# Attention and scan of a four-layer image network as one stream: query chunks of 256 instead of 512, shared 4 KB pieces and shared PSUM banks

## The chip, the cores and the metric

The kernel runs on one core of a Trainium2 chip. A core has a matrix engine (TensorE), an engine for element-wise work and scans (VectorE), one for activation functions (ScalarE), a fourth for general work (GpSimd), a sync engine (SyncE) that issues most transfers, and 16 DMA engines that carry them. Each engine works off its own queue of instructions in the order written; semaphores make one engine wait for another. Operands lie in SBUF, 128 partitions wide; TensorE writes into PSUM, from which VectorE and ScalarE read.

The metric is device microseconds (us) of one execution, the median of the runs.

## The reference, cut to what matters

Four layers work in turn on x of 4 samples x 128 channels x 64 x 64 pixels (4096 positions a sample), all in float32. Only layers 0 and 1 are touched by the change.

```python
# layer 0, per sample: q, v are 128 x 4096; w, b are one number per query position
k      = q / clip(norm(q), 1e-4)
logits = k.T @ q                                   # 4096 keys x 4096 queries
sparse = relu(logits - mean(logits, axis=0) * w + b)
mask   = sparse != 0
attn   = clip(softmax(logits * sparse, axis=0) * mask, 1e-8)
y      = v @ attn                                  # 128 x 4096
x1     = leaky(conv3x3(y) + lin_b) + x

# layer 1, per sample: a selective scan over the 4096 positions, 128 channels x 64 states
u      = layernorm(x_mamba) * gamma + beta
delta  = softplus(dt_raw @ W_dtr + b_dtr)
h[l]   = exp(delta[l] * A) * h[l-1] + delta[l] * B[l] * u[l]
y      = sum_n h[l] * C[l] + u * D
x2     = x1 + (y + silu-gated depthwise conv) @ W_out

# layer 2, per sample: attention with a rank-1 logit, softmax(f_i * g_j), times values
# layer 3: one scan in each direction over all 4 samples' 16384 positions, 256 channels x 16 states
```

## The kernel before, in words

**Order of the program.** The samples run one after the other: `layer0(0)`, `layer1(0)`, `layer0(1)`, `layer1(1)` and so on (`body`, the last function), then layer 2 of the last sample and layer 3. Each stage opens its own pools of SBUF and PSUM and closes them at its end. Nearly every instruction is issued through `InOrder`, whose line L111 the profile therefore shows; it keeps the order on each engine as written. So instructions are told apart by the names of their tiles.

**Layer 0, turns.** A sample's queries are cut into 8 chunks of 512. A *turn* is one block of 256 keys by 512 queries, that is a tile of 128 x 1024 elements (two key blocks of 128 side by side); a chunk has U = 16 turns, a sample S = 128. In turn `i` of the loop these are written, each for a turn of its own, so that they overlap:

- `weights(i)`: VectorE, e = max(t, 0) x lg, reads the logits' PSUM pair.
- `logits(i+2)`: TensorE, two matmuls of 512 columns into one of two PSUM pairs `lg`. A float32 matmul makes two passes of the matrix engine.
- `above(i+1)`: VectorE, t = lg + ncut, the row of thresholds of this chunk.
- `floored(i-18)`: VectorE, t = max(t, fl), where fl is the softmax floor of a chunk, which is known when all 16 turns of the chunk are through: hence the lag of LAG = U + 2 = 18 turns, in which the t tiles are kept.
- `shifted(i)`: GpSimd, e = e - bound; then ScalarE, exp(e). On every second turn ScalarE also takes the sign of a t.
- `beside(i)`: two ScalarE exponentials of 512 with a running sum (`junk`), the row weights of layer 2 of the sample before (not for sample 0).
- `product(i-19)`: TensorE, two matmuls of 512 columns that add into the PSUM tile `acc`.
- `masked(i-1)`: t = mask(t) x e; on odd turns GpSimd, on even turns VectorE.
- `sums(i-2)` on even turns: TensorE adds e over the keys into `zs`.

At a chunk's end `scales` turns zs into the floor and into the scale 1/z: a copy of zs on ScalarE, a matmul with `floor_c` for fl, a small transpose, a reciprocal on VectorE, a spread back by TensorE into `misc`, a copy on ScalarE. `image` multiplies acc by that scale into a padded picture, and `convolved` makes the 3x3 convolution with nine matmuls (taps). `thresholds` make ncut and bound of the next chunk: four matmuls through `misc`, with a ScalarE or VectorE step behind each, and the two steps of bound, one on GpSimd (`top`) and one on VectorE (`top_b`). Convolution, thresholds and values (v) go through a queue: per turn up to two steps that are not TensorE's and one that is.

PSUM (eight banks of 512 float32 columns): two pairs `lg`, and one bank each for `misc`, `zs`, `fl` and `acc`.

After turn S the loop goes on for LAG + 2 turns with only floored, product, image and convolution; beside them runs `first_tokens`, which prepares the first window of layer 1 and stores it (`u1`, `parts1`).

**Layer 1, tiles.** A sample has 4 windows of 1024 positions, each with 64 *tiles* of 128 partitions (16 states of 8 channels) x 1024 positions; 256 tiles a sample. `scan_stream` writes per tile: TensorE's spread of du over the partitions (`db`), ScalarE's decay exp (`da`) from a row that a DMA brings in, VectorE's db x b_rep and the scan itself (`h`), GpSimd's h x c_rep (`p`), and every four tiles TensorE's sums of p into `total`. Of each four tiles one is *apart*: GpSimd makes its x, ScalarE its decay in PSUM. Beside the tiles run, through a queue with `tile` and `late`, the preparation of the next window (`tokens_of`), the depthwise convolution, the finishing of the window before (`done`), layer 2's attention of the sample before (`attend`), and in the last window the queries and keys of the next sample (`tokens`). After the last tile `beside` and the queue are worked off.

Of the kernel before, what the change touches and what calls it, by code (L numbers as in the profile page):

```python
# [16 lines left out]
P = 128  # L17
IMG = 64
# [96 lines left out]

class Net:


    def __init__(self, ctx, tc, ins, out):
# [21 lines left out]
        self.u1 = dram.tile([P, self.T], F32, name="u1", tag="u1")  # L141
        self.parts1 = dram.tile([3, P, self.T], BF16, name="parts1", tag="parts1")
# [160 lines left out]
    def weights12(self):  # L303
# [24 lines left out]
        self.diagD1 = self.diagonals(pool, "diagD1", self.D_param, 1)[:, 0, :]  # L328

# [6 lines left out]
    def layer0(self, b):  # L336
# [4 lines left out]
        NT = L // P  # L341
        U = NT // 2
        S = NCH * U
        LAG = U + 2
        with self.pool("l0", 1) as big, self.pool("l0t", 2) as tmp, self.pool("l0a", LAG + 3) as ap, \
                self.pool("l0e", 4) as ep, self.pool("l0q", 2, True) as ps2, self.pool("l0p", 1, True) as ps1:
            k = big.tile([P, L], F32, name="k", tag="k")
            vT = big.tile([P, NT, P], F32, name="vT", tag="vT")
            ypad = self.padded_image(big, "ypad")
            ksum = self.ksum  # L350

            def misc(name, rows=P):
                return ps1.tile([rows, NB], F32, name=name, tag="misc")

            def row(name, bufs=2, rows=P):
                return tmp.tile([rows, NB], F32, name=name, tag=name, bufs=bufs)

            def pair():
                return ps2.tile([P, 2, NB], F32, name="lg", tag="lg")

            def key(c):
                s = bass.ts(c, NB)
                sp.dma_start(out=k[:, s], in_=self.k0[:, s])

            for c in range(0 if b else NCH):
                s = bass.ts(c, NB)
                xq = row("xq")
                nc.sync.dma_start(out=xq, in_=self.ins["x"][b, :, s])
                ps = pair()
                nc.tensor.matmul(ps[:, 0, :], self.q_wT, xq, start=True, stop=True)  # L370
                q = row("q")
                nc.scalar.activation(q, ps[:, 0, :], AF.Identity, bias=self.q_b)
                nc.sync.dma_start(out=self.q0[:, s], in_=q)
                sq = row("y", 1)
                nc.gpsimd.tensor_tensor(sq, q, q, ALU.mult)
                nc.tensor.matmul(ps[0:1, 1, :], self.ones[:, 0:1], sq, start=True, stop=True)
                own = row("own")
                nc.scalar.activation(own[0:1, :], ps[0:1, 1, :], AF.Sqrt)
                nc.sync.dma_start(out=self.norms[:, s], in_=own[0:1, :])

                n_ps = ps1.tile([P, NB], F32, name="n_ps", tag="zs")
                for i in range(4):
                    nc.tensor.matmul(n_ps[:, i : i + 1], sq[:, bass.ts(i, P)], self.ones[:, 0:1], start=True, stop=True)
                inv = tmp.tile([P, 4], F32, name="inv", tag="inv")
                nc.scalar.activation(inv, n_ps[:, 0:4], AF.Sqrt)
                nc.vector.tensor_scalar(inv, inv, 1e-4, None, ALU.max)
                nc.vector.reciprocal(inv, inv)
                inv_ps = ps1.tile([P, NB], F32, name="inv_ps", tag="fl")
                for i in range(4):
                    nc.tensor.matmul(  # L390
                        inv_ps[:, bass.ts(i, P)], inv[:, i : i + 1].to_broadcast([P, P]), self.ident,
                        start=True, stop=True,
                    )
                nc.vector.tensor_tensor(k[:, s], inv_ps, q, ALU.mult)
                nc.vector.tensor_reduce(ksum[:, c : c + 1], k[:, s], AX.X, ALU.add)
            if b == 0:
                self.weights0()
            kbar = tmp.tile([P, 1], F32, name="kbar", tag="kbar")
            nc.vector.tensor_reduce(kbar, ksum, AX.X, ALU.add)
            nc.vector.tensor_scalar(kbar, kbar, 1.0 / L, None, ALU.mult)  # L400
            kbar_rep = self.replicated(tmp, "kbar_rep", kbar)
            self.exp_tables(act)

            queue = Queue()
            held = {}

            def values(c):
                def load():
                    held["xv"] = row("xq")
                    sp.dma_start(out=held["xv"], in_=self.ins["x"][b, :, bass.ts(c, NB)])  # L410

                def v():
                    held["v"] = misc("v_ps").rearrange("p (a b) -> p a b", b=P)
                    for i in range(4):
                        pe.matmul(held["v"][:, i, :], held["xv"][:, bass.ts(i, P)], self.v_wT, start=True, stop=True)

                def plus():
                    dve.tensor_tensor(
                        vT[:, 4 * c : 4 * c + 4, :], held["v"], self.v_b.unsqueeze(1).to_broadcast([P, 4, P]), ALU.add,
                    )  # L420

                return [load, on_pe(v), plus]

            qs, ncut, bound = {}, {}, {}

            def thresholds(c):


                s = bass.ts(c, NB)

                def load():
                    qs[c] = held["q"] = row("q")
                    sp.dma_start(out=qs[c], in_=self.q0[:, s])
                    held["own"] = row("own")
                    sp.dma_start(out=held["own"], in_=self.norms[:, s].to_broadcast([P, NB]))

                def into(rows, lhsT, key):
                    def go():
                        held["ps"] = misc("th_ps", rows)
                        pe.matmul(held["ps"], lhsT, held[key], start=True, stop=True)  # L440
                    return on_pe(go)

                def hidden():
                    held["h"] = row("h", 1, 64)
                    act.activation(held["h"], held["ps"], AF.Prelu, bias=self.w1_b, alpha=0.2)

                def mean():
                    held["m"] = row("m", 1)
                    act.copy(held["m"], held["ps"])

                def times():
                    dve.scalar_tensor_tensor(held["m"], held["ps"], self.lw2_b, held["m"], ALU.add, ALU.mult)

                def cut():
                    ncut[c] = row("ncut")
                    dve.scalar_tensor_tensor(ncut[c], held["ps"], self.bw2_b, held["m"], ALU.add, ALU.subtract)

                def top():
                    bound[c] = row("bound")
                    pool.tensor_tensor(bound[c], held["own"], ncut[c], ALU.add)  # L460

                def top_b():
                    dve.scalar_tensor_tensor(bound[c], bound[c], 0.0, held["own"], ALU.max, ALU.mult)

                return [
                    load, into(64, self.w1_T, "q"), hidden, into(P, kbar_rep, "q"), mean,
                    into(P, self.lw2_rep, "h"), times, into(P, self.bw2_rep, "h"), cut, top, top_b,
                ]

            def both(t):  # L470
                return t.unsqueeze(1).to_broadcast([P, 2, NB])

            lg, t, e, zs, acc, floor, scale = {}, {}, {}, {}, {}, {}, {}

            def logits(i):
                if i < S:
                    c, m = divmod(i, U)
                    lg[i] = pair()
                    for j in range(2):
                        pe.matmul(lg[i][:, j, :], k[:, bass.ts(2 * m + j, P)], qs[c], start=True, stop=True)  # L480

            def above(i):
                if i < S:
                    t[i] = ap.tile([P, 2, NB], F32, name="t", tag="t")
                    dve.tensor_tensor(t[i], lg[i], both(ncut[i // U]), ALU.add)

            def weights(i):
                e[i] = ep.tile([P, 2, NB], F32, name="e", tag="e")
                dve.scalar_tensor_tensor(e[i], t[i], 0.0, lg.pop(i), ALU.max, ALU.mult)

            def shifted(i):
                if i and i % 2 == 0:

                    act.activation(t[i - 1], t[i - 1], AF.Sign)
                pool.tensor_tensor(e[i], e[i], both(bound[i // U]), ALU.subtract)
                act.activation(e[i], e[i], AF.Exp)

            def sums(i):

                c, m = divmod(i, U)  # L500
                if m == 0:
# [214 lines left out]

# [1365 lines left out]
```

## Time and profile before

Three runs took 10496.26, 10499.89 and 10501.62 us; the median is 10499.89. The profiled execution took 10494.9 us by its span, the time from the first to the last instruction; the page lists no other time of its own, so its execution is set 5.0 us below the median.

| | |
|---|---|
| span of the profiled execution | 10494.9 us, 91078 instructions |
| VectorE busy | 9159.8 us, 87% |
| TensorE busy | 8443.5 us, 80% |
| GpSimd busy | 8156.1 us, 78% |
| ScalarE busy | 6387.1 us, 61% |
| DMA | 1552.75 MB, mean 148 GB/s |

The stages as the starts of tiles show them (layer 0 from the first to the last t <- lg, ncut; layer 1 from the first scan's start to the last's):

| sample | layer 0, from - to (us) | length | gap | layer 1, from - to (us) | length | gap to the next sample |
|---|---|---|---|---|---|---|
| 0 | 63.1 - 686.6 | 623.5 | 99.4 | 786.0 - 1645.0 | 859.0 | 40.0 |
| 1 | 1685.0 - 2323.4 | 638.4 | 100.4 | 2423.8 - 3307.5 | 883.7 | 39.6 |
| 2 | 3347.1 - 3984.5 | 637.4 | 100.6 | 4085.1 - 4966.3 | 881.3 | 39.0 |
| 3 | 5005.3 - 5642.2 | 636.9 | 100.1 | 5742.2 - 6608.9 | 866.7 | |

Layer 2 of the last sample lies between 6609 and 6953 us, layer 3's scans between 6953 and 10415.

How to read what the prediction shows: a group's line gives engine, operation, output <- inputs, partitions x elements, number of instructions, then busy time and mean nanoseconds of one, then the engine's idle time before them and what ended it. A line of a stretch gives, engine by engine, the busy time and in brackets the number of instructions, then TensorE's granted clock (1.0 is full speed), the busy share of the DMA engines and what they moved. A line of the timeline gives the start, the duration, engine and operation. "PE", "DVE", "ACT", "POOL" and "SP" are TensorE, VectorE, ScalarE, GpSimd and SyncE.

### The profile page before, as it was taken

The page shows a single profiled execution, that of the slowest core. Times are in us where ns is not written, and L with a number is a line of the kernel's source. Part 1 is how long each engine was busy: PE and PEld are TensorE (multiplying, and loading weights), DVE is VectorE, ACT ScalarE, POOL GpSimd, SP SyncE. Part 2 cuts the span into 40 slices and gives each one's busy share as a digit, 9 for nine tenths or more (in the row PEclk, how much of TensorE's full clock was granted, in tenths as well). Part 3 has the DMA queues.
Part 4 walks back from the last instruction along what each step waited for, and adds up shares of the span by engine and source line. Part 5 has one row for each costly group of instructions (what it writes and reads, how often), then busy time and mean ns, then how long its engine had stood idle before and what let it go on. Part 6 is the DMA issues. An engine that isn't in the chain of part 4 may idle for free. (4 is left out here: it accounts for less than half of the span.)

```text
span 10494.9 us, 91078 instructions
## 1 busy us (share of the span) xinstructions
PE 8443.5 (80%) x28013; PEld 3021.6 (29%) x28088; DVE 9159.8 (87%) x6318; ACT 6387.1 (61%) x9576; POOL 8156.1 (78%) x3574
## 2 busy tenths in 40 slices
PE   8996667997887997887898887877777777777775
PEld 3331213332223333223333222322222222222221
DVE  7869998887998886999886999359999999999996
ACT  3334545666665665666665776456666666677765
POOL 6758896766887775888674888149999999989986
PEclk9997788998998999998999999888988989888886
DMA  1018882007885005887102888158888888888896
GB/s 37 12 37 201 194 194 85 18 14 189 211 203 149 15 14 129 201 213 191 33 16 63 206 211 200 32 133 199 207 198 206 204 202 208 215 223 224 228 227 176
DMA packets 512313, 1552.75 MB, mean 148 GB/s; under 512 B 84017, under 2 KB 91825, under 8 KB 511825
## 3 DMA queue, kind: packets, MB, share of 16 engines
q1 hardware_dynamic: 511824, 1546.92, 58.9%
q8 instruction: 223, 3.65, 0.2%
q14 instruction: 266, 2.17, 0.1%
HBM read 1349.40 MB, written 137.48 MB: 142 GB/s over the span
## 5 line engine op out<-in xcount | busy, mean ns | idle before, releaser
L111 POOL TENSOR_TENSOR p<-h,c_rep 128x1024 f32<-128x1024 f32 x2048 | 4807.9, 2359 | 734.8 <-DVE h L111 673.7
L111 DVE TENSOR_TENSOR_SCAN h<-da,carry,db 128x1024 f32<-128x1024 f32 x1536 | 3603.4, 2346 | 200.5 <-ACT da L111 17.8
L111 PE MATMUL db<-parts,sel 96*128 96x512 bf16 x4096 | 1401.5, 428 | 1460.3 <-DVE h L111 1408.2
L111 ACT ACTIVATE da<-row,A 128x1024 f32<-128x1024 f32 x1536 | 1761.1, 1147 | 359.4 <-DMA row<-d 341.0
L111 DVE TENSOR_TENSOR db<-b_rep,db 128x1024 f32<-128x1024 f32 x1536 | 1853.5, 1207 | 112.1 <-PE db L111 92.0
L111 POOL TENSOR_TENSOR e<-e,bound 128x1024 f32<-128x1024 f32 x512 | 1241.3, 2427 | 573.5 <-DVE e L111 573.0
L111 POOL TENSOR_TENSOR x<-row,b_rep 128x1024 f32<-128x1024 f32 x512 | 1208.8, 2361 | 123.8 <-DMA row<-d 122.8
L111 DVE TENSOR_TENSOR_SCAN h<-db,carry,x 128x1024 f32<-128x1024 f32 x512 | 1194.9, 2334 | 62.9 <-ACT db L111 35.3
L111 PE MATMUL total<-p,gather 128*32 128x512 f32 x8192 | 1225.7, 719 | 9.8 <-POOL p L111 9.8
L111 ACT ACTIVATE db<-db,A 128x1024 f32<-128x1024 f32 x512 | 555.3, 1085 | 1080.6 <-PE db L111 1026.5
L111 ACT ACTIVATE e<-e 128x1024 f32<-128x1024 f32 x512 | 540.9, 1057 | 1051.9 <-POOL e L111 1051.8
L111 PEld LDWEIGHTS <-sel 96*128 96x128 bf16 x4096 | 309.6, 101 | 3002.0 <-DVE h L111 2017.3
L111 PE MATMUL lg<-q,k 128*128 128x512 f32 x2048 | 1021.5, 623 | 106.5 <-DVE e L111 98.3
L111 PE MATMUL acc<-t,vT 128*128 128x512 f32 x2048 | 964.1, 595 | 3.3 <-DVE t L111 3.3
L111 PE MATMUL acc<-e,values 128*128 128x512 f32 x1536 | 854.9, 648 | 88.8 <-ACT e L111 62.9
L111 DVE TENSOR_TENSOR t<-lg,ncut 128x1024 f32<-128x1024 f32 x512 | 624.5, 1220 | 288.1 <-PE acc L111 264.0
L111 ACT ACT_TABLE_LOAD x617 | 791.6, 1283 | 38.8 <-DMA r<-y 12.3
L111 ACT ACTIVATE e<-gq,below,fcol 128x512 f32<-128x512 f32 x768 | 610.2, 805 | 87.0 <-PE acc L111 86.7
L111 POOL TENSOR_TENSOR t<-t,e 128x1024 f32<-128x1024 f32 x256 | 610.4, 2384 | 45.4 <-ACT t L111 45.4
L111 ACT ACTIVATE junk<-gp,ntop,fcol 128x512 f32<-128x512 f32 x768 | 619.5, 807 | 30.4 <-DMA gp<-g 17.7
L111 ACT COPY carry<-h 128x1 f32<-128x1 f32 x2048 | 373.5, 185 | 416.4 <-DVE h L111 411.4
L111 DVE SCALAR_TENSOR_TENSOR e<-t,lg 128x1024 f32<-128x1024 f32 x512 | 618.5, 1208 | 1.2
(259 smaller groups left out, 9927.5 us busy)
## 6 DMA issues: line engine op xcount, KB each, us to landing
row<-d SPq DMA_DIRECT2D x2048, 512.0 KB
parts<-split SPq DMA_DIRECT2D x912, 64.0 KB
b_rep<-bc SPq DMA_DIRECT2D x96, 512.0 KB
c_rep<-bc SPq DMA_DIRECT2D x96, 512.0 KB
d<-delta SPq DMA_DIRECT2D x76, 384.0 KB
r<-y SPq DMA_DIRECT2D x48, 512.0 KB
xq<-in_x SPq DMA_DIRECT2D x72, 256.0 KB
res<-x SPq DMA_DIRECT2D x32, 512.0 KB
```

Of the source, the lines that this page charges most:

```text
L111: return self.tc.keep_in_program_order(method(*args, **kwargs))
```

## The change

All samples' layers 0 and 1 become one stream (`layers01`). What changes:

- **Memory.** One class, `Memory`, holds SBUF as 44 pieces of 4 KB a partition, which a tile takes and gives back in the order of a queue, and PSUM as two pairs, one bank `a` (misc), one bank `b` and two banks `cd` (the scan's total). In layer 0 acc and fl are the two halves of bank b; zs and the rz of the scale lie in the two banks of cd, in one tile. In layer 1 bank b takes layer 2's acc.
- **Chunks.** A query chunk is Q = 256. A turn is four key blocks of 128 by 256 queries, still 128 x 1024; a chunk has U = 8 turns, a sample still S = 128, and LAG is 10. Thresholds put two results of 256 columns into one bank. The picture is a ring of three padded strips of four rows, whose edges ScalarE copies.
- **Order in a turn.** product, fl's matmul and the two steps of the scale on TensorE now stand ahead of logits; sums follow every turn; the steps of the scale have fixed turns (m = 1 and 2) instead of the queue; thresholds of the next chunk start in turn m = 1 at the head of the queue.
- **Ends beside beginnings.** Turns S and later (floored, product, image, convolution) are written inside the first tiles of layer 1 (`side`). First tokens run in the queue from turn 58, every third turn. The scan begins (rows, first spread) in turn S - 8. The last sums and `done` of the scan before are written in turns 0 to 2 of the next sample's layer 0. Values, keys, mean key, the first chunk's thresholds of the next sample are made in the last window of layer 1; values there get their bias by a matmul with one row and are copied by ScalarE.
- **Beside.** The row weights of layer 2 are exponentials of 1024 from turn 16 on, one a turn and two in each fifth. `attend` starts at tile 21 and doubles up when i % 6 == 2. Layer 1's work of the first window beside the scan starts at tile 16 instead of 2. The nine diagonals of the depthwise convolution are made once and stored.

```diff
+class Memory:
+    def take(self, name, shape=None, dtype=F32):
+        i = self.left.pop(0)
+        t = self.slots.tile(list(shape or [P, self.net.T]), dtype, name=name, tag=f"slot{i}")
...
+    def give(self, *tiles):
+        for t in tiles:
+            self.left.append(self.at.pop(id(t))[0])
...
+        Q = 256
+        NC, RQ, NT = L // Q, Q // IMG, L // P
+        J = self.T // Q
+        U = NT // J
+        S = NC * U
         LAG = U + 2
...
+        def sums(i):
+            m = i % U
+            if "zs" not in bank:
+                both_banks = mem.total("zs_rz")
+                bank["zs"], bank["rz"] = both_banks[:, 0:Q], both_banks[:, NB:]
...
+        def floored(i):
+            dve.tensor_tensor(t[i], t[i], both(bank["fl"]), ALU.max)
...
+        def floor_of(c):
+            if "b" not in bank:
+                bank["b"] = mem.other("acc_fl")
+                bank["acc"], bank["fl"] = bank["b"][:, 0:Q], bank["b"][:, Q:]
+            pe.matmul(bank["fl"], self.floor_c, zcopy.pop(c), start=True, stop=True)
...
+        def turn_of(i):
+            c, m = divmod(i, U)
+            w = i - LAG
...
+            if i in due:
+                d = due.pop(i)
+                image(d)
...
+            if i < S:
+                weights(i)
+            if 0 <= w - 1 < S:
+                product(w - 1)
...
+            if 0 <= w < S and w % U == 0:
+                floor_of(w // U)
+            scaled = U < i <= S + 2
+            if scaled and m == 1:
+                run[0][1]()          # turned
+            if scaled and m == 2:
+                run[0][3]()          # spread
+            logits(i + 2)
+            above(i + 1)
+            if 0 <= w < S:
+                floored(w)
+            if scaled and m == 1:
+                run[0][2]()          # inverted
+            if i and i <= S and (i - 1) % 2:
+                signs(i - 1)
+            if i < S:
+                shifted(i)
+            beside(i)
+            if scaled and m == 2:
+                run[0][4]()          # copied
+            if 0 < i <= S:
+                masked(i - 1)
+                for o in range(0 if i == 3 else i - 1, i) if i >= 3 else ():
+                    sums(o)
+            if i and i <= S and i % U == 0:
+                run[0] = scales(i // U - 1)
+                run[0][0]()          # kept
+            if i < S and m == 0 and c + 1 < NC:
+                given(c + 1)
+            if m == 1:
+                if i < S and c + 1 < NC:
+                    queue.first(thresholds(c + 1))
...
+            rounds(2 if i < LAG else 1)
...
+    def layers01(self):
...
+            for b in range(self.B):
+                after = self.layer0(b + 1, mem) if b + 1 < self.B else None
+                prior, Y = Y, self.layer1(b, mem, Z, after)
+                for i in range(Z.S):
+                    if prior and i == 0:
+                        prior.scan.last()
...
+                    if i >= 58 and i % 3 == 1:
...
+                        if early:
+                            Z.queue.add(early.pop(0))
+                    if i == Z.S - 8:
+                        Y.scan.begin()
+                    Z.front(i)
+                Y.scan.ready()
+                for i in range(Y.scan.n):
+                    Y.scan.tile(i)
+                if after:
+                    after.start()
+                    Y.kept["queue"] = after.queue
...
+            tail = kept["before"]
+            if tail:
+                tail.tail(tail.S + i)
+                tail.rounds(1)
+                if tail.over():
+                    tail.close()
+                    kept["before"] = None
             beside(i)
...
         net.weights012(pool)
-        for b in range(net.B):
-            net.layer0(b)
-            net.layer1(b)
+        net.layers01()
```

(The four words behind # name the steps that `scales` returns and are not in the code.)

## The prediction

> **What bounds the kernel now.** I read four views: the stretches of each stage, the groups of VectorE and GpSimd in one attention stage, the groups of VectorE in one scan stage, and the order of time inside an attention stage.
>
> ```profile
> core 0: us, PE busy (x) PEld busy (x) DVE busy (x) ACT busy (x) POOL busy (x), PEclk, DMA share, GB/s
> 1645.00:1695.00 50.00, 31.15 (x81) 10.89 (x80) 24.44 (x39) 10.51 (x20) 11.17 (x9) 0.80 0.41 138
> 1700.00:2320.00 620.00, 575.66 (x1729) 225.16 (x1730) 537.99 (x454) 411.93 (x706) 452.00 (x196) 0.98 0.05 15
> 2323.00:2430.00 107.00, 81.14 (x226) 34.02 (x225) 42.79 (x49) 36.17 (x49) 17.49 (x13) 0.90 0.32 84
> 2430.00:3300.00 870.00, 704.22 (x2575) 254.44 (x2577) 830.28 (x521) 598.52 (x919) 752.74 (x329) 0.92 0.84 208
> ```
>
> These are sample 1's stages. In the scans (2430 to 3300) VectorE is busy 95%: it is the bound, and what is added to it there is paid. In the attention (1700 to 2320) TensorE has 93% and VectorE 87%. In the 107 us and 50 us between, VectorE is busy 40 to 50%: that is what the change goes for. From the starts of the rows t<-lg and h<-da,carry,db: layer 0 runs 63.1-686.6, 1685.0-2323.4, 3347.1-3984.5, 5005.3-5642.2 (sum 2536); layer 1 runs 786.0-1645.0, 2423.8-3307.5, 4085.1-4966.3, 5742.2-6608.9 (sum 3491); the four gaps from 0 to 1 sum to 400, the three from 1 to 0 to 119. The rest of the 10494.9 us span is not touched.
>
> ```profile
> L111 DVE TENSOR_TENSOR t<-lg,ncut 128x1024 f32<-128x1024 f32 x122 | 148.8, 1220 | 73.4 <-PE acc L111 66.1 <-PE lg L111 7.3
> L111 DVE TENSOR_TENSOR t<-t,fl 128x1024 f32<-128x1024 f32 x108 | 130.5, 1209 | 1.3 <-PE fl L111 1.3
> L111 DVE SCALAR_TENSOR_TENSOR t<-t,e 128x1024 f32<-128x1024 f32 x61 | 102.8, 1685 | 6.0 <-ACT e L111 6.0
> L111 DVE SCALAR_TENSOR_TENSOR bound<-bound,own 128x512 f32<-128x512 f32 x7 | 18.5, 2649 | 0.0
> L111 POOL TENSOR_TENSOR e<-e,bound 128x1024 f32<-128x1024 f32 x123 | 297.6, 2421 | 133.4 <-DVE e L111 133.4
> L111 POOL TENSOR_TENSOR t<-t,e 128x1024 f32<-128x1024 f32 x61 | 145.4, 2383 | 11.2 <-ACT t L111 11.2
> ```
>
> Today t<-t,fl hardly waits (1.3 us in 108). The two VectorE operations with both inputs in SBUF, t<-t,e and bound, take 1.69 and 2.65 us on average although one of 1024 elements needs 1.2: they stand still while a GpSimd operation runs.
>
> ```profile
> 302.63 2.12 DVE L111 SCALAR_TENSOR_TENSOR t<-t,e 128x1024 f32<-128x1024 f32 x1
> 303.07 1.88 PE L111 MATMUL acc<-t,vT 128*128 128x512 f32 x4
> 311.06 1.16 PE L111 MATMUL rz_ps<-ident,rzt 128*128 128x128 f32 x8
> 313.05 1.22 DVE L111 SCALAR_TENSOR_TENSOR t<-t,e 128x1024 f32<-128x1024 f32 x1
> ```
>
> Four passes of 512 columns last 1.88 with a last one of 0.59, so 0.43 each; eight of 128 last 1.16 with 0.29, so 0.12 each. A pass of 256 is then 0.215 to 0.23. In the same view VectorE starts a 1024 operation every 1.13 us, one of 256 about every 0.35; GpSimd one of 1024 every 2.35; ScalarE's e<-e lasts 1.06.
>
> **The change, part by part.** I call one 128x1024 block of attention a turn; a sample has 128, as before, but a chunk is now 8 turns, not 16.
>
> 1. Gaps. 0 to 1: left are the rest of the last turns (3.4 to 6 us of VectorE), a selection matmul and a db product, so 10 each (bounds 4 and 20): 400 becomes 40, **-360**. 1 to 0: scan 2.3, GpSimd's p 2.4, the queued bound steps 1.1 and t<-lg 1.2, so 7 (3 to 15): 119 becomes 21, **-98**.
>
> 2. The attention's end in the scans. Ten t<-t,fl at 1.13, two images at 0.35 and some 5 of waits in the first tiles, where the scale's short steps pass through four engines: 17 a sample (12 to 30), all on VectorE and so on the path: **+68**. Its products (1.7 of TensorE a turn) lie under a scan tile's 3.4 us.
>
> 3. The scan's end in the first ten turns. These have no product and no t<-t,fl yet; GpSimd needs 2.35 + 2.35/2 = 3.5 a turn. The last window's finish brings 6.7 of VectorE and 5.3 of TensorE with waits of one for the other: 4.5 a turn (3.6 to 6), 45 in all, 44 for sample 0.
>
> 4. First tokens in turns 58 to 127. VectorE: two t minus split (the helper `less`), each 1.13 plus up to 2.3 behind GpSimd, and short ones: 7. All their matmuls share bank a with thresholds and convolution, each waiting for ScalarE to empty it: 18 more by eight chunks at about 2. So 25 (7 to 60).
>
> 5. The turn itself, other 117. TensorE: 16 passes at 0.215 for lg and acc, two groups of sums at 0.215 and two changes of operand at 0.1: 4.1; a chunk adds taps 3.9, thresholds 2.1, floor and scale 1.3: 40.2 per chunk, 5.0 a turn. VectorE: 24 operations at 1.13, four t<-t,e at 1.13, three of them held 1.2 by GpSimd, four of 256 at 0.35: 36.7, or 4.6 a turn. So neither load reaches today's 5.03 (638.4 / 127). The waits are what is new:
>  - zs and rz are one tile now. The built program makes the row sums of turn 2 wait until ScalarE has copied rz, behind that turn's exp: e<-t 1.2, e minus bound 2.4, exp 1.1, junk 1.4 (a 1024 row with 0.19 of read-out; two of 512 are 2.0), copy 0.4 = 6.5 after the turn's start. Then Prelu and mean, so the second threshold pair ends at 8.2, and the next turn's product, behind it in TensorE's queue, at 10.1. VectorE reached t<-t,fl at 6.8. Loss 3.3 a chunk, 1.9 for sample 0 (no junk).
>  - That t<-t,fl waits at all for a product comes from acc and fl being halves of one bank: in the built program each t<-t,fl waits for the product before it. 1.3 a chunk more, where TensorE is behind (turns 2 and 7).
>  - The GpSimd and the VectorE step of bound are issued in the same turn, an even one, where GpSimd first does e minus bound and t<-t,e: 2.35 + 2.35 + 0.65 after e<-t, while VectorE is through at 3.4: 3.3 a chunk, in which the whole queue of VectorE stands.
>  Sum 36.7 + 7.9 = 44.6, 5.6 a turn; sample 0 43.2, 5.4. Bounds: today a chunk of 16 turns takes 82.5 us (16 x 5.16 in mid-stage) against 79.0 of TensorE by the same passes, 4% over; TensorE's 5.0 with that 4% is 5.25, the lower end. If the queues never catch up and each wait costs twice, the turn is 36.7 + 15.8 over 8, 6.5; I put the range's end half-way, at 6.0. I take 5.6, since each of the three waits stands in the built program.
>  Layer 0: 44 + 117 x 5.4 + 25 = 701; the others 45 + 117 x 5.6 + 25 = 725: 2876 for 2536, **+340**.
>
> 6. Small: nine diagonals before the start, **+3** (today 2.8 a sample, in a gap). Values with bias rows and copies move to ScalarE in the last window: 7 of TensorE and 4.5 of ScalarE, under VectorE's scans; all paid it would be 11 a sample. Twice as many small transfers a chunk on SP: the DMA share in that stage is 0.05; uncovered, they would hold thresholds that have five turns of lead. Shared 4 KB pieces: the scans in the built program wait for the same producers as today, and GpSimd's p less often for TensorE; 0.1 a tile either way would be 100 in all.
>
> TensorE's passes decide part 5. The Trainium skill (TensorE: Matmul & The Clock Gate, Back-to-back issue gap) has 81 ns for 128 columns and 131 for 512 in real streams, which would make a pass of 256 half again as dear as half of one of 512. By it, an estimate, the turn would be 7.4 and the time near 11,300. The rows above, where 128 columns cost 0.12 and 512 cost 0.43, decide for the smaller price.
>
> Sum: -360 - 98 + 68 + 340 + 3 = **-47**. The profiled execution is 10494.9, the runs' median 5 above it; I add 5: 10,453, say 10,450.
>
> **Rivals.**
> - Faster still (0.2): the waits are absorbed by the slack between the queues, as t<-lg's 0.6 a turn is today, and the turn falls to TensorE's load, 5.25: 351 x -0.35 + 117 x -0.15 = -140, 10,310. For it: both loads are under 5.1. Against: each wait has a whole chain of four engines in order before it.
> - Slower (0.25): bank a. In turns 58 to 127 the first threshold pair waits until ScalarE, after exp and junk, has emptied the bank of a token or convolution step; 3 to 4 us in each of 35 chunks, carried on into the 3.3 above. Part 4 then costs 60 and not 25 a sample: +140, 10,590. It decides from 37 a sample on.
> - Slower (0.13): shared pieces. Row loads or scan outputs wait for a piece that is not free; 0.1 a tile, +100, 10,550. Against: the built program's waits.
>
> **How the numbers follow.** What a measurement can tell from no change is 0.2%, 21 us: faster means under 10,479, slower over 10,521. My case, a small gain, has 0.3 and the fast rival 0.2: 0.5 faster. 0.12 between, where part 5 is 0.1 a turn worse than computed (468 turns). Slower 0.38 by the two rivals or by a turn of 5.8 and more. Since signs are mixed: my case alone spans 10,380 to 10,479; the range of 8 in 10 goes from the fast rival, 10,310, to a turn of 6.0, 468 x 0.4 = 187 over, 10,640.
>
> **What will show it.** Gaps between last t<-lg and first scan under 20 us (else part 1 is wrong). The attention's turn between 5.3 and 5.7. VectorE's t<-t,acc_fl idle before it, on TensorE, by 4 to 5 us a chunk; bound idle on GpSimd by 3. Scan tiles as today but for the first ten. I am wrong if turns stay near 5.2 or pass 6, or if scan tiles change.

## The result, and the profile after

The changed kernel takes 10668.51 us (median, 10663.87 to 10675.88) against 10500.57 for the kernel before: a ratio of 1.016, 95% interval 1.0146 to 1.0175. It is slower by 168 us, where a gain of 50 was forecast, and 28 us above the stated range. The profiled execution spans 10662.1 us, 167 more than the one of before.

Taken apart at the starts of the same rows as before (layer 0 from the first to the last t<-lg, layer 1 from the first to the last scan, summed over four samples):

| part | before | after | difference | predicted |
|---|---|---|---|---|
| start of the first turn | 63 | 51 | -12 | +3 |
| layer 0, 4 x 128 turns | 2536 | 3019 | +483 | +340 |
| gaps from layer 0 to 1 | 400 | 38 | -362 | -360 |
| layer 1, tiles 0 to 31 | 452 | 508 | +56 | +68 |
| layer 1, tiles 192 to 255 | 867 | 956 | +89 | 0 |
| layer 1, the tiles between | 2172 | 2172 | 0 | 0 |
| gaps from layer 1 to 0 | 119 | 18 | -101 | -98 |
| layers 2 and 3 after that | 3886 | 3900 | +14 | 0 |

Both kinds of gap went as far as forecast. What came back was larger: layer 0's turns by 143, the scans' last window by 89.

The stretches of sample 1 in the changed kernel (turns; gap; scans up to 3300 us; the last two dozen scans; gap), with TensorE's granted clock after the busy times:

```profile
core 0: us, PE busy (x) PEld busy (x) DVE busy (x) ACT busy (x) POOL busy (x), PEclk, DMA share, GB/s
1710.00:2465.00 755.00, 670.45 (x3504) 477.57 (x3505) 555.24 (x532) 396.19 (x567) 468.43 (x219) 0.96 0.08 22
2469.00:2479.00 10.00, 7.10 (x47) 3.84 (x45) 9.23 (x9) 3.79 (x4) 9.76 (x4) 1.00 0.42 105
2480.00:3300.00 820.00, 676.14 (x2548) 265.85 (x2552) 784.12 (x504) 561.49 (x874) 693.61 (x308) 0.93 0.84 208
3300.00:3399.00 99.00, 94.81 (x346) 44.24 (x344) 76.05 (x45) 50.98 (x79) 69.49 (x33) 0.84 0.65 165
3399.00:3406.00 7.00, 5.05 (x22) 3.63 (x20) 4.41 (x5) 1.31 (x6) 4.08 (x3) 1.00 0.00 0
```

In the turns no engine is full any more: TensorE falls from 93% to 89%, VectorE from 87% to 74%. They wait for each other. In the scans VectorE has its 95.6% until 3300, then 77% while TensorE has 96%: there the bound has changed hands.

VectorE's groups in the same turns, idle time before them last:

```profile
L112 DVE TENSOR_TENSOR t<-lg,rows 128x1024 f32<-128x1024 f32 x127 | 154.5, 1216 | 3.2 <-PE lg L112 3.2
L112 DVE TENSOR_TENSOR t<-t,acc_fl 128x1024 f32<-128x1024 f32 x115 | 140.0, 1217 | 135.7 <-PE acc_fl L112 134.7
L112 DVE SCALAR_TENSOR_TENSOR rows<-rows,rows 128x256 f32<-128x256 f32 x15 | 6.4, 424 | 45.1 <-POOL rows L112 45.1
```

The idle time sits where it was looked for: 135.7 us before t<-t,acc_fl, on TensorE (8.5 for each of 16 chunks, forecast 4.6 without the first tokens), and 45.1 before VectorE's 15 steps of bound (the row rows<-rows,rows), 3.0 each, on GpSimd (forecast 3.3). Before t<-lg, where the kernel before had 73 us, there are 3. Where the wait stands is one thing; which cause is worth what, the runs had to tell.

### The profile page after: what moved, and what is told of

Same layout as the page of the kernel before. It is cut to its first block, busy times and chain, and to the rows that moved or that the text cites. A ratio compares the mean times of both kernels' runs of the same rounds, so it can differ in the third digit from the quotient of the medians.

```text
span 10662.1 us, 105733 instructions
## 1 busy us (share of the span) xinstructions
PE 8610.2 (81%) x35245; PEld 4096.6 (38%) x35320; DVE 9095.0 (85%) x6427; ACT 6236.6 (58%) x9105; POOL 8159.6 (77%) x3638
## 5 line engine op out<-in xcount | busy, mean ns | idle before, releaser
L112 POOL TENSOR_TENSOR p<-h,rep 128x1024 f32<-128x1024 f32 x1024 | 2404.3, 2356 | 574.3 <-DVE h L112 514.2
L112 POOL TENSOR_TENSOR p<-h,c_rep 128x1024 f32<-128x1024 f32 x1024 | 2404.4, 2359 | 306.7 <-DVE h L112 285.3
L112 POOL TENSOR_TENSOR e<-e,rows 128x1024 f32<-128x1024 f32 x512 | 1215.3, 2374 | 1038.9 <-DVE e L112 956.7
L112 PE MATMUL lg<-rows,k 128*128 128x256 f32 x4096 | 1028.9, 396 | 155.3 <-DVE e L112 146.6
L112 DVE TENSOR_TENSOR t<-t,acc_fl 128x1024 f32<-128x1024 f32 x512 | 622.6, 1216 | 560.3 <-PE acc_fl L112 556.3
L112 PE MATMUL acc_fl<-t,vT 128*128 128x256 f32 x4096 | 1042.6, 399 | 30.8 <-DVE t L112 18.1
L112 DVE TENSOR_TENSOR db<-b_rep,db 128x1024 f32<-128x1024 f32 x768 | 927.3, 1207 | 57.3 <-PE db L112 57.3
L112 DVE TENSOR_TENSOR db<-rep,db 128x1024 f32<-128x1024 f32 x768 | 928.0, 1208 | 23.4 <-PE db L112 22.8
L112 PEld LDWEIGHTS lg<-rows,k 128*128 128x128 f32 x4096 | 784.0, 197 | 324.9 <-issue 132.3
L112 PEld LDWEIGHTS acc_fl<-t,vT 128*128 128x128 f32 x4096 | 774.8, 196 | 281.6 <-issue 96.8
```

The source lines that it names most:

```text
L112: return self.tc.keep_in_program_order(method(*args, **kwargs))
```

## Experiments

Each edit stands alone on the changed kernel (10,668) unless the text says what it is added to. "Less" and "more" are differences of medians from different sessions, in which the kernel before took between 10,501 and 10,512; a difference of some 12 us is therefore no finding. Times of VectorE in "turns 18 to 56 of sample 1" are for 38 turns, 218.5 us in the changed kernel and 194.5 before.

**VectorE's step of bound one turn later.**

```diff
-            return [on_pe(first), hidden, mean, on_pe(second), times, cut, top, top_b]
+            return [on_pe(first), hidden, mean, on_pe(second), times, cut, top] + ([] if c else [top_b])
...
                 pool.tensor_tensor(bound[c], own[c], ncut[c], ALU.add)
+                if c:
+                    tops.append(top_b)
...
+            while tops:
+                tops.pop()()
             rounds(2 if i < LAG else 1)
```

> VectorE's step of bound is issued one turn later than GpSimd's, so that VectorE does not stand behind GpSimd's e minus bound and t<-t,e. In the changed kernel it stood 16.5 us before 5 of these in turns 16 to 58 of sample 1, 3.3 each, 60 in all. Theory of added waits (the three waits of a chunk stand one after the other on the path): -3.3 x 60 = -198, about 10,470. Rival, the load of TensorE's queue: VectorE only arrives earlier at t<-t,acc_fl and waits there for the product; less than 60 us gained, above 10,610, and the idle time before t<-t,acc_fl grows by what the other lost.

Measured: 10,539 (ratio to before 1.0036, 1.0022 to 1.0049), 129 less; layer 0 loses 133, 2.2 for each of 60 chunks. Changed kernel and experiment, VectorE's groups in turns 16 to 56:

```profile
L112 DVE TENSOR_TENSOR t<-t,acc_fl 128x1024 f32<-128x1024 f32 x40 | 48.7, 1216 | 28.0 <-PE acc_fl L112 27.3
...
L112 DVE SCALAR_TENSOR_TENSOR rows<-rows,rows 128x256 f32<-128x256 f32 x5 | 2.1, 425 | 16.5 <-POOL rows L112 16.5
```

```profile
L112 DVE TENSOR_TENSOR t<-t,acc_fl 128x1024 f32<-128x1024 f32 x40 | 48.7, 1218 | 38.7 <-PE acc_fl L112 37.8
...
L112 DVE SCALAR_TENSOR_TENSOR rows<-rows,rows 128x256 f32<-128x256 f32 x5 | 2.1, 417 | 0.0
```

The 16.5 us before bound are gone, and 10.7 of them stand before t<-t,acc_fl instead: these 40 turns are only 5.6 us shorter (222.3 after 227.9). Turns 58 to 127 of the same sample, which hold the first tokens, are 25 us shorter (412.5 after 437.8), so that over the whole of layer 0 two thirds of the forecast are kept. Neither theory had it: the wait was on the path, at a third of its price in one stretch and nearly all of it in the other.

**zs, rz and fl apart from each other and fl apart from acc.** The two banks of layer 1's total become two tiles of one bank (`third` and `fourth`). In layer 0 one holds zs, the other rz and fl; only the last chunk's fl, which is read beside layer 1's first tiles, stays in acc's bank.

```diff
-                both_banks = mem.total("zs_rz")
-                bank["zs"], bank["rz"] = both_banks[:, 0:Q], both_banks[:, NB:]
+                bank["zs"], bank["d"] = mem.third("zs")[:, 0:Q], mem.fourth("rz_fl")
+                bank["rz"], bank["fl"] = bank["d"][:, 0:Q], bank["d"][:, Q:]
...
-                bank["acc"], bank["fl"] = bank["b"][:, 0:Q], bank["b"][:, Q:]
+                bank["acc"] = bank["b"][:, 0:Q]
+            if c == NC - 1:
+                bank["fl"] = bank["b"][:, Q:]
```

> The two banks of zs and rz become two tiles, fl goes from acc's bank into rz's (only the last chunk's stays with acc), so the row sums of turn 2 no longer wait for ScalarE's copy of rz and t<-t,fl no longer for the product before it. VectorE's idle time before t<-t,acc_fl in turns 16 to 58 was 32.6 us in 5.5 chunks, 5.9 a chunk. Theory of added waits: most of it goes, 4.6 to 5.9 a chunk over 62 chunks, -285 to -365, but not below TensorE's 5.25 a turn, so -235: about 10,430. Rival, TensorE's load: turns stay above 5.5 and less than 60 us are gained, since logits, one place behind the product in its queue, come no earlier.

Measured: 10,515 (1.001, 1.0001 to 1.002), 153 less; layer 0 takes 2871 instead of 3019. That lies between the two theories, and the edit moves two things at once; the next two runs separate them.

**zs and rz apart, acc and fl left together.**

```diff
-                both_banks = mem.total("zs_rz")
-                bank["zs"], bank["rz"] = both_banks[:, 0:Q], both_banks[:, NB:]
+                bank["zs"], bank["rz"] = mem.third("zs")[:, 0:Q], mem.fourth("rz")
```

> The part of the last but three runs that splits zs from rz alone (acc and fl stay halves of one bank). Both together gave 10,515, 153 less than the change. My sum had 3.3 a chunk for the zs/rz wait and 1.3 for the acc/fl wait, 72 to 28: by it about -110, 10,558, and t<-t,acc_fl still waits 1 to 2 us a chunk. Rival: the acc/fl pair is the larger, since fl's reader t<-t,fl then waits for the whole product in every turn: then less than 60 is gained here, above 10,608.

Measured: 10,680 (1.016, 1.0145 to 1.0175): nothing gained. A wait that I had priced at 3.3 a chunk, as high as any, was worth nothing. TensorE's waits in turns 16 to 56, changed kernel first, then this run (what waited, on whom, total, times, longest):

```profile
PE zs_rz L112 <- ACT rows L112: 9.4, 8, 2.1
```

```profile
DVE t L112 <- PE acc_fl L112: 28.9, 21, 5.7
...
PE rz L112 <- ACT rows L112: 5.5, 5, 2.0
...
PE th_ps L112 <- ACT rows L112: 3.9, 3, 2.2
```

The 9.4 us were 5.5 for zs's copy, which stay, and 3.9 for rz's copy, which now stand one step further on in TensorE's queue, before the second pair of thresholds: these need ScalarE's Prelu and mean, right behind rz's copy. VectorE's 28.9 before t<-t,acc_fl are those of the changed kernel (27.3).

**fl apart, with the wait for rz's copy kept.** Its row sums take their ones from a small tile that ScalarE rewrites behind that copy.

```diff
                 act.copy(scale[c], bank["rz"][:, 0:Q])
+                act.copy(bank["one"], self.ones[:, 0:32])
...
-                    bank["zs"][r : r + P // J, :], self.ones[:, 0 : P // J], e[i][:, j, :],
+                    bank["zs"][r : r + P // J, :], bank["one"], e[i][:, j, :],
```

> As the run with zs, rz and fl apart (10,515), but the row sums' matmul takes its ones from a small tile that ScalarE rewrites right behind the copy of rz, so turn 2's row sums wait for that copy again as in the change. Splitting zs from rz alone gained nothing (10,680). If the bank of acc and fl carries the whole effect, this stays within 30 of 10,515. If the two waits cover each other, so that only both gone together help, it goes back to 10,620 or more.

Measured: 10,526 (1.0021, 1.0011 to 1.0031), within the 30 us. The other wait was there: in turns 16 to 56 TensorE's row sums stood 6.2 us in all, five times, for the rewritten tile. So fl's place alone is worth 142 us with that wait (10,668 to 10,526) and 165 without it (10,680 to 10,515). VectorE in turns 16 to 56 of this run:

```profile
L112 DVE TENSOR_TENSOR t<-lg,rows 128x1024 f32<-128x1024 f32 x40 | 48.6, 1216 | 8.9 <-PE lg L112 8.9
L112 DVE TENSOR_TENSOR t<-t,rz_fl 128x1024 f32<-128x1024 f32 x40 | 48.5, 1212 | 16.6 <-PE rz_fl L112 16.6
```

The Trainium skill (PSUM — Partial Sum Buffer, PSUM bank collisions raise a hardware error) has it that accesses of two engines to the same bank and the same 32 partitions must be ordered, reads and writes alike, even where the columns are disjoint. The changed kernel's waits are of that kind: t<-t,acc_fl reads one half of a bank and waits for matmuls into the other. No run here shows a collision itself; what the order costs in this kernel is the difference above.

**The values' bias in one matmul.** 512 columns at once, ahead of the values.

```diff
+                    if on_act:
+                        pe.matmul(
+                            held["v"], self.ones[0:1, :], self.v_b[0:1, :].unsqueeze(1).to_broadcast([1, 4, P]),
+                            start=True, stop=False,
+                        )
                     for i in range(4):
...
-                        if on_act:
-                            pe.matmul(held["v"][:, i, :], self.ones[0:1, :], self.v_b[0:1, :], start=False, stop=True)
```

> In the last window the values' bias is one matmul of 512 columns a step instead of four of 128 between the values. A step took 3.3 us of TensorE (16 passes of 128 at 0.207, because operands alternate), eight steps 26 a sample, in which VectorE stood 23 us. Price theory: 2 passes at 0.43 and 8 at 0.11 to 0.2 are 1.8 to 2.5, so 0.8 to 1.5 less in each of 8 steps, 3 samples: -20 to -36, 10,630 to 10,650; the last 32 tiles then take 117 to 123 us instead of 129. Rival, the queue that is let on in every tile: the same number of steps, so nothing changes.

Measured: 10,635 (1.0128, 1.0113 to 1.0143), 33 less; samples 1 and 2 take 112.9 us for the last 32 tiles instead of 128.9 (107.7 before). TensorE's groups for the values in the last window of sample 1, changed kernel and experiment:

```profile
L112 PE MATMUL v_ps<-v_b,ones 1*128 1x128 f32 x64 | 18.6, 376 | 0.0
...
L112 PE MATMUL v_ps<-v_wT,xv 128*128 128x128 f32 x64 | 17.6, 363 | 0.1
```

```profile
L112 PE MATMUL v_ps<-v_wT,xv 128*128 128x128 f32 x64 | 11.1, 326 | 0.0
L112 PE MATMUL v_ps<-v_b,ones 1*128 1x512 f32 x16 | 10.0, 707 | 0.2 <-ACT vT L112 0.2
```

36.2 us of TensorE against 21.1; the granted clock in the two stretches, 0.87 and 0.91, would by its ratio explain under 2 of these 15. Over the three windows concerned the profiled run gains 46 us in tiles 192 to 255, of which layer 0 gives 15 back (3034 after 3019); no run shows why. How it reaches VectorE, from the order of time in the changed kernel (ScalarE, then VectorE):

```profile
3374.45 0.59 ACT L112 COPY vT<-v_ps 128x512 f32<-128x512 f32 x1 [7.13 <-PE v_ps L112]
3374.93 0.20 ACT L112 COPY carry<-h 128x1 f32<-128x1 f32 x1
3375.03 1.15 ACT L112 ACTIVATE da<-row,A 128x1024 f32<-128x1024 f32 x1
3378.22 1.09 ACT L112 ACTIVATE db<-db,A 128x1024 f32<-128x1024 f32 x1 [2.04 <-PE db L112]
```

```profile
3379.39 2.35 DVE L112 TENSOR_TENSOR_SCAN h<-db,carry,x 128x1024 f32<-128x1024 f32 x1 [7.49 <-issue]
```

ScalarE's copy of the values waits 7.1 us for the matmuls, and the carry and both decays of the next tiles stand behind it in the queue: VectorE's scan, for whose wait the profile names no releaser, starts 0.1 us after the second of these decays has ended, 7.5 us after VectorE's last work.

**Layer 2's exponentials ahead of exp on ScalarE.**

```diff
+            beside(i)
             if i < S:
                 shifted(i)
-            beside(i)
```

> ScalarE's exponentials with a sum for layer 2 (1.4 us each, two in each fifth turn) are issued ahead of e minus bound's exp and not behind it, where the copies of zs, rz, thresholds and first tokens stand behind them. ScalarE waited 106 us of 240 for GpSimd before that exp, so they lie in idle time there. Theory of added waits, with ScalarE late in the chain: rz's copy, Prelu and the tokens' copies come 1.4 to 2.8 earlier, two of them on the path in a chunk: 2.8 to 4 a chunk x 45 chunks of three samples: -126 to -180, about 10,520; sample 0, which has no such exponentials, stays at 739. Rival, the wait is TensorE's or GpSimd's: within 30 us of 10,668.

Measured: 10,555 (1.0051, 1.0034 to 1.0068), 114 less, and all of it in samples 1 to 3: their layer 0 takes 720 to 724 instead of 760, sample 0 does not gain (745 after 739). VectorE's idle time before t<-t,acc_fl in turns 16 to 56 falls from 28.0 to 19.3, and TensorE's wait for ScalarE's copies of zs and rz from the 9.4 above to 2.4:

```profile
DVE t L112 <- PE acc_fl L112: 18.6, 18, 2.8
...
PE zs_rz L112 <- ACT rows L112: 2.4, 5, 0.7
```

So the place of the copies behind these exponentials is a cause of TensorE's lateness, and it is worth more than the zs/rz wait through which I had counted it. As with bound, the stretch with the first tokens gains most: 28 us of sample 1's 40.

**First tokens after the last turn.**

```diff
-                    if i >= 58 and i % 3 == 1:
...
                     Z.front(i)
+                for run in Y.first_tokens():
+                    Z.queue.add(run)
+                while Z.queue:
+                    Z.queue.step()
+                Y.scan.begin()
```

> First tokens of layer 1 run after the last turn, as a stretch of their own, and the scan's first loads after them. If they are what makes turns 56 to 104 6.3 to 6.6 us long (310 in sample 1 against 48 x 5.75 = 276), these turns fall to 270 to 280, 34 less a sample, and the gap grows by what the tokens take alone, 60 to 90 (with the tail it was 100 before): 10,770 to 10,890. If their matmuls in bank a cost 60 a sample, as the rival in the prediction had it, the turns fall by 60. If the excess has another cause, the turns stay and the time is 10,900 or more.

Measured: 10,740 (1.0217, 1.0202 to 1.0232). Turns 56 to 104 of sample 1 fall from 310 to 275, the whole of layer 0 by 35 to 41 a sample (the scan's first loads, moved too, included), and each gap grows from 9.5 to 64 to 66. So beside the turns the first tokens are still cheaper, by 18 a sample in the time; but they cost 35 to 41 there, not 25.

What one of them does, in the changed kernel's order of time:

```profile
2219.37 1.24 ACT L112 ACTIVATE junk<-gp,ntop,fcol 128x1024 f32<-128x1024 f32 x1
...
2220.61 0.67 ACT L112 ACTIVATE bcd<-c_ps,b_cd 72x512 f32<-72x512 f32 x1
...
2221.33 2.07 PE L112 MATMUL de_ps<-bcd,W_dtr 8*128 8x512 f32 x2 [4.14 <-ACT bcd L112]
...
2223.33 3.73 PE L112 MATMUL acc_fl<-t,vT 128*128 128x256 f32 x8
...
2227.10 1.22 DVE L112 TENSOR_TENSOR t<-t,acc_fl 128x1024 f32<-128x1024 f32 x1 [6.72 <-PE acc_fl L112]
```

TensorE waits 4.1 us for ScalarE, which has two exponentials of layer 2 in front; then its own passes take twice their time (product 3.73, usually 1.89), and VectorE, bound to the product by the shared bank, stands 6.7 us.

**Two waits, four edits, and two more.** Bound later with zs, rz and fl apart; then these with one bias and the exponentials ahead.

> Bound one turn later and zs, rz, fl apart from each other and from acc (the runs that gave -129 and -153 alone). If they stand one after the other on the path, -282: 10,386, and turns 18 to 56 go from 218 to about 195 us (5.15 a turn). If they cover each other or a load takes over: turns not below 5.4, above 10,440.

> All four at once: bound later, zs, rz and fl apart, one bias matmul, layer 2's exponentials ahead of exp. Additive: -129 -153 -33 -114 = -429, 10,240. TensorE's load (5.0 a turn and 4%, 5.25): layer 0 would be 4 x (45 + 117 x 5.25 + 25) = 2737 instead of 3019, -282, and -33: 10,353. I expect the second, 10,330 to 10,380, under the kernel before by 1.2 to 1.6%.

Measured: 10,418 (0.9911, 0.9895 to 0.9928) and 10,313 (0.981, 0.9795 to 0.9824). Bound later and the banks apart nearly add up (-129 and -153 alone, -251 together), though turns 18 to 56 of sample 1 take 203.5 and not 195. All four give -356, where the single ones sum to -429, and are faster than the 10,330 that was expected at best: turns 18 to 56 stop at 194.9 in samples 1 to 3 (194.8 in sample 0). The stretch that holds them in the run with all four:

```profile
core 0: us, PE busy (x) PEld busy (x) DVE busy (x) ACT busy (x) POOL busy (x), PEclk, DMA share, GB/s
1728.00:1932.00 204.00, 200.91 (x1113) 149.81 (x1111) 186.02 (x166) 128.60 (x187) 147.46 (x69) 1.00 0.04 11
```

TensorE has 98.5%: 5.02 us a turn of load and 5.1 of time. So next to no waiting of TensorE is left there to take away, and the turn is that of the kernel before (194.5 for 38 turns).

Two edits to sample 0's start on top of these. First one TensorE step a turn from the queue, not two:

```diff
-            rounds(2 if i < LAG else 1)
+            rounds(2 if b and i < LAG else 1)
```

> The run with all four edits (10,312), and in sample 0's first ten turns the queue gives one TensorE step a turn, as the kernel before does, and not two. There ten turns took 75 us against 46 before and 50 in the other samples: the second values step of a turn waits in bank a until VectorE, in its own order, has emptied the first. If that is the cause, the ten turns fall to 50 to 58: 10,285 to 10,297. If it is values' loads or the thresholds, they stay at 75 or what is put off comes back later: 10,312.

Measured: 10,295 (0.9799, 0.9785 to 0.9814); sample 0's first ten turns 62 instead of 75, 13 less where 17 to 25 were expected, though the time lies in the range given. TensorE's wait for the values' load was still there, so that load was brought forward:

```diff
+            values = [Z.values(u, False) for u in range(L // self.T)]
+            for steps in values[0:2]:
+                steps.pop(0)()
             diag = mem.fixed("diag1", [P, 9, P], "taps")
             self.weights12(diag)
```

> As the run with all four edits and one step (10,295), and the first two loads of sample 0's values are issued ahead of the later layers' weights, of which A alone is 48 small transfers that keep SyncE's queue busy for 18 us. In the change TensorE stood 22.7 us for this load in sample 0's first turns, and in the run before still 22.8. If this load is what is left, the first ten turns fall from 62 to 45 to 50 and the time by 12 to 20: 10,275 to 10,283. If what is shifted back behind it is needed as early, or GpSimd and the thresholds are as late, nothing is gained: 10,290 to 10,300.

Measured: 10,283 (0.978, 0.9767 to 0.9794), ten turns in 54.3, 8 less. The wait for the load is gone, and TensorE now waits for VectorE to empty bank a, which may be why ten turns are not at 50. The changed kernel, then this run:

```profile
PE v_ps L112 <- DMA xv<-in_x: 22.7, 1, 22.7
```

```profile
PE v_ps L112 <- DVE vT L112: 17.7, 3, 15.0
```

So of the 22.7 us that TensorE stood for the load, only 8 came back in these turns. This is the fastest version: 2.2% under the kernel before, from the same change with the waits named above taken out or shortened.

## Why the prediction was wrong, point by point

- **Part 1, the gaps**: right, -362 and -101 for -360 and -98.
- **Part 2, the attention's end in the scans**: right in size, 11 to 17 a sample where 17 stood.
- **Part 3, the first ten turns**: too small. 45 was forecast, 51 to 52 came; sample 0 had 72 for 44. Neither the second TensorE step a turn nor the values' load stood in the sum; on the version with all four edits, where the ten turns took 75, taking the step away gave 13 us and bringing the load forward another 8, and 10 over the forecast stay unexplained. Part 3 is 47 us short in all. The 12 us by which the first turn starts earlier, not forecast either, set against them.
- **Part 4, first tokens**: 25 forecast, 35 to 41 by the run that moves them out, 54 us in all. The rival "bank a" had 60 a sample and a deciding point of 37: the truth lies at that point. It named half of the mechanism, TensorE held by ScalarE behind its exponentials; but in turns 58 to 127 of sample 1 only one pair of thresholds waits so for the bank (3.4 us), while 10 us in three places are waits of the tokens' own matmuls for results that ScalarE has yet to write, as with bcd above. What I left out of part 4 is that a held TensorE holds VectorE too, through acc and fl.
- **Part 5, the turn**: right as a sum, but by luck, and wrong as an explanation. The load of TensorE was right (5.0 a turn forecast, 5.02 in the run with all four). Without first tokens (the run that moves them out) the 117 turns take 5.40 in sample 0 (forecast 5.4) and 5.71 in the others (5.6), 39 us over. But of the three terms one of the two largest, the 3.3 a chunk of "zs and rz are one tile now", is worth nothing, and the smallest, the 1.3 of "acc and fl being halves of one bank", is worth 2.4 (142 us in the 58 chunks of 468 turns). Bound's 3.3 is worth 2.2. The step that failed is to follow one chain to its victim and put the price on the first wait in it. The row sums' wait and the thresholds' stood one behind the other for the same engine, so taking away the first leaves the second; what handed TensorE's lateness to VectorE was the shared bank. ScalarE's exponentials in front of the copies, which the sum held only as 1.4 a chunk inside the row sums' wait, are worth 114 us, 2.5 in each of 45 chunks. That terms too large and too small came out near the sum is no merit of the reasoning.
- **Part 6, the last window**: the failed term of the scans. "7 of TensorE" for the values was 36.2. 7 is 64 passes of 128 columns at the 0.11 of like passes in a row; there are 128, they alternate between two pairs of operands, and they took 0.28 each at a granted clock of 0.87. "Under VectorE's scans" failed too. All paid it was to be 11 a sample; samples 0 to 2 paid 27 to 32. The run with one bias matmul gives 14 to 16 of these back, and the trace shows the way, the copies in ScalarE's queue ahead of the decays; the other 11 to 18 no run takes apart.
- **Shared 4 KB pieces**: right; tiles 32 to 191 take the same time.

Sum: 47 + 54 + 39 + 89 - 12 (part 2) - 15 (start) + 14 (layers 2 and 3) - 4 (gaps) = 212 of the 214 between forecast (-47 on the span) and trace (+167). No rival reached the time either, since the largest of them was one mechanism, and four parts (3, 4, 5 and 6) were too small at once.

Not settled: why the first ten turns of samples 1 to 3 take 10 to 11 us more than before, and the 14 us in layers 2 and 3, which stay, to a few us, in every version.

## What to carry to other kernels

When two results move into one PSUM bank, look for the reader that now waits for the other result's writer, in every turn and not only at the chunk's end; that pairing cost 142 us here. A wait is worth what the next wait in the same queue does not take over, so before pricing the first, name what stands right behind it and for whom. And a step moved "under" the bound engine is covered only if nothing of it stands in a queue ahead of what feeds that engine.

## What the runs showed that was not expected

- A TensorE that had stood for 4.1 us came back at half its clock. Three stretches of the changed kernel around the wait shown above:

```profile
2204.00:2221.00 17.00, 10.99 (x62) 6.77 (x60) 13.05 (x14) 7.32 (x12) 9.36 (x5) 0.97 0.00 1
2221.00:2227.00 6.00, 5.67 (x11) 3.46 (x12) 0.00 (x0) 5.95 (x8) 3.09 (x2) 0.51 0.10 22
2227.00:2237.00 10.00, 9.69 (x53) 6.56 (x52) 8.11 (x7) 4.50 (x6) 3.40 (x2) 1.00 0.08 20
```

  The granted clock is 0.51 for the six us behind the wait and 1.00 after. The Trainium skill (TensorE: Matmul & The Clock Gate, What's actually happening) puts the halving at an idle window of about 3.4 us; this wait, a little longer, agrees, and so do the waits of 4.13 us in samples 2 and 3 (0.51 and 0.53 behind them). But the length alone does not decide in this trace: a wait of 2.09 us at 3435 us was followed by 3 us at 0.50, one of 3.35 us at 3782 by 6 us at 1.00. So the wait shown cost its length and again about 3 us of slow passes. In sum this matters: in turns 58 to 127 of sample 1 the granted clock averages 0.96 in the changed kernel, 0.97 to 0.98 with bound later, with zs, rz and fl apart or with the exponentials ahead, and 1.00 with all four. How much of an edit's gain is a wait and how much the clock behind it, no run separates.
- With bound's wait gone, VectorE's t<-t,e grew from 1753 to 1829 ns on average in turns 16 to 56, and to 2118 with all four edits: the tighter turn seems to put more of them beside a GpSimd operation, which no run separates.
